# Routing of the last block in fewer stages and ahead of other work, shared weights in ten loads, all layer 2 keys ahead of layer 1's norm

## The chip, the cores and the metric

The kernel runs on one core of a Trainium2 chip. The metric is the device time of one execution in microseconds (us). The core has a matrix engine (TensorE, PE in the profile; PEld is its loading of weights), a vector engine (VectorE, DVE), a scalar engine for activation functions (ScalarE, ACT), GpSimd (POOL) and a sync engine (SP) that here issues most of the DMA transfers. Each engine runs its own instructions in order and waits on semaphores for the others.

## The reference

The input x is f32 of 16 sequences of 128 tokens with 256 features; a context of the same shape feeds the attentions. Four layers follow one another, each a gated cross-attention and a gated feed-forward part:

```
x = x + tanh(g_xattn[i]) * attention_i(layernorm(x), context)
x = x + tanh(g_ffn[i])   * ffn_i(layernorm(x))
```

Three of the feed-forward parts choose 2 of 8 experts for every token (a mixture of experts, MoE). Cut to what matters:

```python
# layer 0: gelu experts, 256 -> 1024 -> 256
gate = softmax(x @ w_gate.T);  scores, idx = top_k(gate, 2)
out  = sum over the two of  scores * (gelu(x @ W1[e] + b1[e]) @ W2[e] + b2[e])
# layer 1: one dense layer with low-rank additions weighted by a softmax
# layer 2: like layer 0 with swiglu experts of 512, chosen by softmax + gate_b, and
#          a shared expert that every token goes through
# layer 3: silu(x @ gate[e]) * (x @ up[e]) @ down[e], weights of the two normalised
```

## The kernel before, in words

**Tiles and blocks.** A sequence (128 tokens) fills the 128 partitions. Four sequences form a block, so there are four blocks, 0 to 3 (`NBLK = 4`, `BPB = 4`, `B = 16`).

**Routing.** `Moe.front` (L436) is the routing of one block: the norm (`ln_block` L316, with `inverse_sd` L221 for 1/sd and `normalized` L299), transposes of the normalised rows (`ps_ln`, L329), the router's product (L413), a softmax, the first choice and the second (`first_max`, each some six DVE operations on 128x32), their sum `both` (L464), two matmuls that rank the tokens of each expert (L469, L470), the weights of the choices (L476 to L502), the row numbers (`off` to `xi`, L505 to L521) and eight scatters by POOL of rows into a table in HBM (`xg`, L524). The running count of tokens per expert, `self.carry`, goes from block to block. `plan` (L592) then works out which expert each slot of 128 rows belongs to; SP reads it into registers (L714).

**Slots.** A slot of an MoE loads 128 rows (`xr`, L753) and, when the expert is a new one, its weights (`fetch`, L1374); without a new expert the load is issued and skipped. PE transposes the rows (L786), does the first products (L1421 in layer 0, L1598 in layer 2, L1646 in layer 3), then the second (L823), and the result is scattered by POOL (L835). Layer 0 does its first slots from a plan of blocks 0 and 1, layer 3 from a plan of blocks 0 to 2, while the attention of later blocks is still going on; the rest come from block 3's plan.

**The order by hand.** `attend` (L1303) emits the work of PE, ACT and DVE in an order written out by hand (`tc.manual_schedule`); the queues of SP and POOL are ordered by a planner. Routing, keys and the like are generators (`jobs`). At each `tick()` every job whose count has run out does its next stage; a stage ends at a `yield n`, and n is the number of ticks until the next one. Once the last scores are out, `late` is true and n is cut to 1, unless it is a `Firm` number, which is kept. At that point the `filler` begins too: early slots in layers 0 and 3, the shared expert of blocks 0 to 2 in layer 2 (`shared2`, L1522; products L1533 and L1555). The filler comes last at every tick. The routing of block 3 is the job that starts last (`jobs.append` after the last `att.output`) and runs beside it.

```python
        def tick():
            for job in list(jobs) + filling:
                job[1] -= 1
                if job[1] <= 0:
                    try:
                        n = next(job[0])
                        job[1] = n if isinstance(n, Firm) else min(n, most[late])
```

**Keys and shared weights.** Layers 1 and 2 run in one `attend`. The keys of both (`keys`, L1144; product L933, eviction by ACT at L1152) need only the context. Ahead of layer 1's first norm stand keys of layer 1's blocks 0 and 1 and of layer 2's blocks 0, 1 and 2; layer 2's block 3 is made with layer 1's next block. The four key tiles of layer 2 and the five tiles of the shared expert's weights use five buffers of one pool (`shared_tile`, L1505), so a weight's load waits until the scores of its buffer's keys are done. `load_shared` starts these five loads of 512 KB in the first step of layer 2's last block.

Of the kernel before, what the change touches and what calls it, by code (L numbers as in the profile page):

```python
# [12 lines left out]
ALU = mybir.AluOpType  # L13
# [6 lines left out]
P = 128  # L20
B = 16
# [69 lines left out]
def kernel(ctx: ExitStack, tc: tile.TileContext, a: dict, out: bass.AP):  # L91
# [112 lines left out]
    class Firm(int):  # L204
        pass

    def quick(job):

        for n in job:
            yield min(n, 3)  # L210
# [105 lines left out]
    def ln_block(blk, see=None, own_set=False):  # L316


        mv, rstd = yield from ln_residual(blk, own_set=own_set)
        if see is not None:  # L320
            see(rstd)
        xns = yield from normalized([xs[b] for b in block(blk)], mv, rstd)
        yield Firm(3) if own_set else 4
        xt = xtpool.tile([P, KC, TB], F32, tag="xnT", name="xnT")
        for pair in range(BPB // 2):
            ps = ps_x.tile([P, KC, 2 * S], F32, tag="x", name="ps_ln")
            for j in range(2):
                for k in range(KC):
                    nc.tensor.transpose(  # L329
                        ps[:, k, j * S:(j + 1) * S],  # L330
                        xns[:, pair * 2 + j, k * P:(k + 1) * P], ident,
                    )
            nc.scalar.copy(xt[:, :, pair * 2 * S:(pair + 1) * 2 * S], ps)
            yield 1 if pair == 0 else 3
        return xns, xt

    def gated_bias(bias_row, gate):
# [34 lines left out]
    def small(tag, w=NE):  # L372
        return rpool.tile([P, BPB, w], F32, tag=tag, name=tag)
# [48 lines left out]
    class Moe:  # L422
# [4 lines left out]
        def __init__(self, layer, wg, turn, see=None):  # L427
            self.layer, self.wg, self.turn, self.see = layer, wg, turn, see
            self.carry = region
            self.done = None  # L430
            self.scatters, self.returns, self.weighted = [], [], []

        def kept(self, shape, tag, dtype=F32):
            return rpool.tile(shape, dtype, tag=tag, name=tag, bufs=NBLK)

        def front(self, blk, plan=None):  # L436
# [25 lines left out]
            first_max(hot[:, 1], key2)  # L462
            both = small("both")
            nc.vector.tensor_tensor(both, hot[:, 0], hot[:, 1], ALU.add)  # L464
            yield Firm(2) if own_set else 6


            ps = ps_x.tile([P, 2, BPB, NE], F32, tag="x", name="ps_rank")
# [31 lines left out]
            )  # L500
            nc.vector.tensor_copy(xns[:, :, D + 1], cg[:, 1])
            nc.vector.tensor_tensor(xns[:, :, D + 2], cg[:, 0], cg[:, 1], ALU.subtract)  # L502
            yield 3
            off = small("off")
            nc.vector.tensor_copy(off[:, 0], self.carry)  # L505
            for i in range(1, BPB):
# [2 lines left out]
            nc.vector.tensor_tensor(  # L509
                self.carry, off[:, BPB - 1], ps[:, 1, BPB - 1], ALU.add  # L510
            )
            at = small("at")
            nc.vector.tensor_tensor(at, off, ps[:, 0], ALU.add)
            where = rpool.tile([P, 2, BPB, NE], F32, tag="where", name="where")
# [11 lines left out]
                        out_offset=bass.IndirectOffsetOnAxis(ap=xi[:, j, i:i + 1], axis=0),  # L526
                    ).ins, self.scatters, "scatter")
            if plan is not None:
                yield 1
                yield from plan()  # L530
            return xnT

        def last(self, pool):
# [55 lines left out]
                )  # L589
            made.append(ins)  # L590

        def plan(self, turns, early=False, kind=""):  # L592

# [2 lines left out]
            def t(shape, tag, dtype=F32):  # L598
# [1 line left out]

            have = t([P, NE], "have")
            nc.vector.scalar_tensor_tensor(
                have, self.carry, float(1 - P if early else 0), region, ALU.add, ALU.subtract
            )
            full = t([P, NE, B], "past")
            nc.vector.tensor_tensor(
# [15 lines left out]
                cnt = left  # L622
            else:
                nc.vector.tensor_scalar(skip, cnt, -1.0, float(B), ALU.mult, ALU.add)
            yield 1
            part = t([P, NE, NE], "part")
            nc.vector.tensor_tensor(
                part, below, cnt[:, None, :].to_broadcast([P, NE, NE]), ALU.mult
# [5 lines left out]
                past, iota[:, :n, None].to_broadcast([P, n, NE]),  # L634
                end[:, None, :].to_broadcast([P, n, NE]), ALU.is_ge,
            )
            yield 1
            eid = t([P, n], "eid")
            nc.vector.tensor_reduce(eid, past, AX.X, ALU.add)
            nc.vector.tensor_tensor(  # L640
# [1 line left out]
            )  # L642
            ahead = t([P, n], "ahead")
            nc.vector.tensor_reduce(ahead, past, AX.X, ALU.add)
            yield 1
            plan = t([P, 4, n], "plan")

            nc.vector.tensor_scalar(plan[:, 0], eid, float(NE - 1), None, ALU.min)
# [5 lines left out]
            else:  # L654
                nc.vector.tensor_tensor(at, ahead, iota[:, :n], ALU.add)
            nc.vector.tensor_scalar(plan[:, 1], at, float(P), None, ALU.mult)
            yield 1

            nc.vector.tensor_tensor(
                plan[:, 2, 1:], plan[:, 0, 1:], plan[:, 0, :n - 1], ALU.not_equal  # L660
# [8 lines left out]
            nc.vector.tensor_copy(plan_i, plan)  # L669
            code = t([P, n], "code" + kind)  # L670
            nc.vector.tensor_scalar(code, plan[:, 0], -1.0, float(NE), ALU.mult, ALU.add)
            yield 1
            if early:

                upto = t([P, NE], "upto")
# [423 lines left out]
    class Fast16:  # L1099
# [30 lines left out]
        def prepare(self, blk, before):  # L1130


            made = [self.queries(blk, before)]
            if blk not in self.kT:
                made.append(self.keys(blk))
            if self.others is not None:

                if blk == 0:
                    made.append(self.keys(1))
                for later in (0, 1, 2) if blk == 0 else (3,) if blk == 1 else ():  # L1140
                    made.append(self.others.keys(later))
            return made

# [156 lines left out]
        mybir.EngineType.PE, mybir.EngineType.Activation, mybir.EngineType.DVE  # L1300
    }

    def attend(parts, most=(99, 1), filler=None, open_end=False):  # L1303

# [27 lines left out]
        with tc.manual_schedule(engines=IN_ORDER):  # L1334
            ln_exp()
            prepared = ahead(*blocks[0][:2], 0)
            for n in range(len(steps) + 2):
                if n == len(steps) - 1 and open_end:
                    next(filler)
                if n == len(steps):  # L1340
                    late = True
                    if filler is not None:
                        filling.append([filler, 0])
                if n < len(steps):
                    if n % BPB == 0:

                        while any(job in jobs for job in prepared):
                            tick()
                        if n // BPB + 1 < len(blocks):
                            att, before, _, blk = blocks[n // BPB + 1]  # L1350
                            prepared = ahead(att, before, blk)
                    att, b = steps[n]
                    att.scores(b, tick)
                if 1 <= n <= len(steps):
                    att, b = steps[n - 1]
                    att.values(b, tick)
                if n >= 2:
                    att, b = steps[n - 2]
                    att.output(b, tick)
                    if b % BPB == BPB - 1:  # L1360
                        _, _, behind, blk = blocks[(n - 2) // BPB]
                        jobs.append([behind(blk), 0])
            while jobs or (filling and not open_end):
                tick()

# [139 lines left out]
    def shared_tile(pool, name):  # L1505
        return pool.tile([P, KC, TB], F32, tag="shared", name=name, bufs=5)

    def shared_weights(pool):

        sw = []  # L1510
        for name in ("l2_w1", "l2_w3"):
            for half in range(2):
                t = shared_tile(pool, "sw")
                nc.sync.dma_start(
                    out=t, in_=a[name][NE, :, half].rearrange("(k p) f -> p k f", p=P)
                )
                sw.append(t)
        w2 = shared_tile(pool, "sw2").rearrange("p k (c d) -> p (k c) d", d=D)
        nc.sync.dma_start(out=w2, in_=a["l2_w2"][NE].rearrange("(c p) d -> p c d", p=P))
        return [*sw, w2]  # L1520

    def shared2(weights, bias, blk, xnT, get):  # L1522

# [563 lines left out]
    def layers(fast):  # L2087
# [11 lines left out]
        def right(stack, name):  # L2099
            return stack.enter_context(tc.tile_pool(name=name, bufs=1, side="right"))  # L2100
# [3 lines left out]
        def routed(moe, turns, begin=None):  # L2104


            plans = []

            def make(blk):
                early = blk < NBLK - 1  # L2110
                kind = str(len(plans)) if early else ""
                plans.append((yield from moe.plan(turns[blk], early, kind)))
                if early and begin is not None:
                    begin(plans[-1])

            def behind(blk):
                if blk in turns:
                    job = moe.front(blk, lambda: make(blk))
                    yield from quick(job) if blk < NBLK - 1 else job
                else:  # L2120
                    yield from moe.front(blk)

            return behind, plans

        def cycle(lanes, n, at=0):
            return [lanes[(at + i) % len(lanes)] for i in range(n)]

        bufs0 = {"xr": 6, "hT": 2, "bias": 2}
        with tc.tile_pool(name="context", bufs=1) as cpool, ExitStack() as for_mid:
# [100 lines left out]

            plans = []

            def load_shared(blk):

                if blk == NBLK - 1:
                    sw.extend(shared_weights(spool))
                yield 1

            def front2(blk):
                def make():  # L2240
                    plans.append((yield from moe2.plan(cycle((2, 1, 0), NSLOT))))

                xnTs.append((yield from moe2.front(blk, make if blk == NBLK - 1 else None)))

            with tc.tile_pool(name="mid", bufs=2) as pool:
                lora = Lora(pool, wpool, biases["base_b"])
# [12 lines left out]
                else:  # L2259
                    parts = [shifted(pool, layer, w, ctxT) for layer, w in zip((1, 2), ws)]  # L2260
                parts = [
                    (parts[0], lambda blk: moe.fetch(pool, blk), lora.run),
                    (parts[1], load_shared, front2),
                ]

                def most_shared():
# [7 lines left out]
                        yield from shared2(sw, biases["sb"], blk, xnTs[blk], get)  # L2274

                if fast:
                    attend(parts, filler=most_shared())
                else:
                    for att, before, behind in parts:
                        general(att, None if att.layer == 2 else before, behind)  # L2280
        with ExitStack() as for_last:
            with tc.tile_pool(name="ffn2", bufs=2) as pool:
                if not fast:
                    sw.extend(shared_weights(right(for_shared, "shared")))
                get = tiles(pool, BUFS2)
                with for_shared, tc.tile_pool(name="hidden", bufs=2) as hpool:
                    def get_shared(tag, shape):
# [150 lines left out]
```

## Time and profile before

| | us |
|---|---|
| median of 11 runs (lowest, highest) | 1657.24 (1654.4, 1660.22) |
| the profiled execution | 1658.69 |
| its span, first to last instruction | 1656.8 |
| mean granted TensorE clock | 0.971 of full speed |

| stretch, us from the start | what runs | PE busy | clock | DMA share |
|---|---|---|---|---|
| 0 to 150 | layer 0 attention | 126.2 of 150 | 0.94 | 0.57 |
| 150 to 235 | block 3's routing, early slots, hand-over | 78.8 of 85 | 0.98 | 0.73 |
| 235 to 415 | layer 0's slots | 180.0 of 180 | 1.00 | 0.42 |
| 415 to 716 | layer 1, layer 2 attention | 281.3 of 301 | 0.96 | 0.14 |
| 716 to 870 | shared expert, block 3's routing, hand-over | 149.6 of 154 | 1.00 | 0.22 |
| 870 to 1480 | layer 2's slots, layer 3 attention | 598.5 of 610 | 0.99 | 0.23 |
| 1480 to 1560 | block 3's routing, early slots, hand-over | 65.1 of 80 | 0.91 | 0.55 |
| 1560 to 1657 | layer 3's slots, end | 60.0 of 97 | 0.83 | 0.61 |

All times are those of one profiled execution. "Busy" is the time in which an engine was at work, the clock is what the throttle granted to TensorE in that stretch, and the DMA share is the mean busy share of the core's 16 DMA engines. In lines of a timeline, the number in brackets is how long the engine had been idle before, and after the arrow stands what ended that wait.

### The profile page before, as it was taken

To read this page: it belongs to the slowest core of one execution; us is meant where nothing else is said; L and a number is where in the kernel's file an instruction comes from. 1 tells how busy PE (TensorE), PEld (TensorE's weight loads), DVE (VectorE), ACT (ScalarE), POOL (GpSimd) and SP (SyncE) were. 2 spreads that over 40 slices of the span, in tenths; PEclk is the share of its full clock that TensorE was granted. 3 is DMA by queue.
4 is the path that set the end of the run, shared out by engine and by line. 5 is a ranking of instruction groups with operands and counts; after the bars stand their busy time and mean duration, and the time that the engine had idled before them with its cause. 6 is when DMAs were issued, how large, how long until landed. Compare 5 with 4: busy or idle time off the path is not lost.

```text
span 1656.8 us, 34913 instructions
## 1 busy us (share of the span) xinstructions
PE 1539.5 (93%) x12803; PEld 1193.2 (72%) x12803; DVE 875.8 (53%) x2850; ACT 637.5 (38%) x1517; POOL 327.8 (20%) x412
## 2 busy tenths in 40 slices
PE   6988999999889999999999999999989999998891
PEld 4677889999455666655559999999846665677791
DVE  3776322422367766764445555556724535557664
ACT  4545423345355555453225333334443323222110
POOL 4133411111600000221100111011150002023433
PEclk9999999999999999999999999999999999999996
DMA  9606575342600000110065413310260000034855
GB/s 340 229 31 221 175 259 177 120 145 89 118 2 1 1 14 15 40 40 26 26 208 161 151 43 135 121 33 28 97 121 1 14 1 27 1 119 135 275 181 174
DMA packets 111272, 169.68 MB, mean 102 GB/s; under 512 B 17129, under 2 KB 84526, under 8 KB 111088
## 3 DMA queue, kind: packets, MB, share of 16 engines
q1 hardware_dynamic: 86224, 112.38, 21.6%
q0 software_dynamic: 20304, 49.66, 9.6%
q10 hardware_dynamic: 4560, 5.25, 1.0%
q8 instruction: 108, 1.77, 0.4%
q14 instruction: 76, 0.62, 0.1%
HBM read 268.81 MB, written 48.18 MB: 191 GB/s over the span
## 4 chain that ended last, share of the span: by engine, by line
PE 76%; DVE 10%; DMA 6%; ACT 4%; issue 1%; POOL 1%; SPq 1%; DVEq 0%; ACTq 0%
PE ps_w L1598 16%; PE ps_e L823 12%; PE ps_h L1421 7%; PE ps_w L1533 6%; PE ps_qk L1855 4%; PE ps_v L1964 3%; PE ps_o L1267 3%; PE ps_s L1212 2%; PE ps_g L1646 2%; PE ps_k L933 2%; DVE rs L1278 2%; PE ps_q L933 2%; PE ps_u L1646 2%; PE ps_s L1985 2%; PE ps_y L2031 2%; PE ps_s L1555 2%
## 5 line engine op out<-in xcount | busy, mean ns | idle before, releaser
L1598 PEld LDWEIGHTS ps_w<-xT,w 128*128 128x128 f32 x2304 | 264.0, 192 | 2.5
L1598 PE MATMUL ps_w<-xT,w 128*128 128x128 f32 x2304 | 264.9, 275 | 0.0
L835 POOL DMA_INDIRECT yd<-y,to x117 | 119.5, 1021 | 561.0 <-DVE c L798 306.6
L823 PE MATMUL ps_e<-w,hT 128*128 128x256 f32 x848 | 197.6, 380 | 2.4 <-DVE hT L1503 1.3
L823 PEld LDWEIGHTS ps_e<-w,hT 128*128 128x128 f32 x848 | 154.5, 190 | 21.6 <-DVE hT L1503 2.3
L1606 ACT ACTIVATE u<-ps_w,b 128x128 f32<-128x128 f32 x312 | 89.4, 368 | 172.3 <-PE ps_w L1598 165.0
L1609 DVE SCALAR_TENSOR_TENSOR m<-ps_w,b,u 128x128 f32<-128x128 f32 x312 | 87.8, 344 | 111.0 <-PE ps_w L1598 94.0
L1421 PE MATMUL ps_h<-xT,w 128*128 128x128 f32 x1120 | 133.5, 278 | 7.1 <-DMA w<-in_l_w_dram 4.3
L1421 PEld LDWEIGHTS ps_h<-xT,w 128*128 128x128 f32 x1120 | 131.4, 194 | 10.5 <-issue 3.7
L1426 ACT ACTIVATE hT<-ps_h,b 128x128 f32<-128x128 f32 x312 | 89.3, 374 | 114.5 <-issue 79.5
L524 POOL DMA_INDIRECT xg<-xn,xi x96 | 94.3, 983 | 153.7 <-ACT u L1539 55.0
L1533 PE MATMUL ps_w<-xnT,sw 128*128 128x512 f32 x256 | 111.9, 593 | 0.0
L831 DVE SCALAR_TENSOR_TENSOR y<-ps_e,c,bias 128x256 f32<-128x256 f32 x78 | 37.6, 482 | 125.7 <-PE ps_e L823 124.5
L1081 POOL TENSOR_TENSOR sum_range<-sum_range,rs 128x256 f32<-128x256 f32 x48 | 35.2, 733 | 342.1 <-DVE rs L1278 156.7
L1533 PEld LDWEIGHTS ps_w<-xnT,sw 128*128 128x128 f32 x256 | 47.9, 190 | 57.3 <-issue 50.9
L1278 DVE RECIPROCAL rs<-ps_o 128x256 f32<-128x256 f32 x32 | 56.2, 1756 | 44.6 <-PE ps_o L1267 43.1
L788 DVE COPY xT<-ps_xr 128x256 f32<-128x256 f32 x117 | 48.5, 417 | 58.3 <-PE ps_xr L786 58.2
L306 ACT ACTIVATE xn<-x,nmr,rstd 128x256 f32<-128x256 f32 x128 | 67.8, 597 | 29.2 <-DVE nmr L302 29.2
L1212 PE MATMUL ps_s<-qM,kT 32*128 32x256 f32 x768 | 71.2, 431 | 5.1 <-ACT e L1227 5.0
L1227 ACT ACTIVATE e<-ps_s 128x512 f32<-128x512 f32 x128 | 65.7, 601 | 12.1 <-PE ps_s L1212 12.0
L815 ACT ACTIVATE bias<-b,c 128x256 f32<-128x256 f32 x78 | 40.4, 518 | 70.5 <-DVE c L801 26.5
L1212 PEld LDWEIGHTS ps_s<-qM,kT 32*128 32x128 f32 x768 | 40.8, 194 | 33.5 <-issue 19.0
(276 smaller groups left out, 2580.2 us busy)
## 6 DMA issues: line engine op xcount, KB each, us to landing
w<-in_l_w_dram SPq DMA_DIRECT2D x156, 1024.0 KB
w<-in_l_w_dram SPq DMA_DIRECT2D x39, 512.0 KB
kT<-in_l_wgu_dram SPq DMA_DIRECT2D x39, 512.0 KB
xg<-zeros POOLq DMA_DIRECT2D x15, 1170.0 KB, 24.8
xr<-xg SPq DMA_DIRECT2D x78, 130.0 KB
b<-in_l_b_dram SPq DMA_DIRECT2D x78, 128.0 KB
kT<-in_l_w_dram SPq DMA_DIRECT2D x39, 256.0 KB
x<-yd POOLq DMA_DIRECT2D x48, 128.0 KB, 4.8
```

The costliest lines, as they stand in the source:

```text
L306: nc.scalar.activation(xns[:, i, 0:D], src, AF.Identity, bias=nmr[:, i:i + 1], scale=rstd[:, i:i + 1])
L524: self.unordered(nc.gpsimd.indirect_dma_start(out=xg[:, :], in_=xns[:, i, :], in_offset=None, out_offset=bass.IndirectOffsetOnAxis(ap=xi[: ...
L823: nc.tensor.matmul(po, lhsT=hT[:, f, :], rhs=lane(s)["w2"][:, f, :], start=(f == 0), stop=(f == nf - 1),)
L835: self.unordered(nc.gpsimd.indirect_dma_start(out=yd[:, :], in_=y, in_offset=None, out_offset=bass.IndirectOffsetOnAxis(ap=to[:, 0:1], axi ...
L1212: nc.tensor.matmul(pss[j][:, 2 * c:2 * c + 2, :], lhsT=self.kT[blk][part, c, tok], rhs=self.qM[blk][part, c, :, tok], start=True, stop=True,)
L1278: nc.vector.reciprocal(rs, po[:, 1])
L1421: nc.tensor.matmul(ps[:, i, :], lhsT=w["w1"][:, k, f * P:(f + 1) * P], rhs=xT[:, k, :], start=(k == 0), stop=(k == KC - 1),)
L1426: nc.scalar.activation(hT[:, f, :], ps[:, i, :], AF.Gelu, bias=w["b1"][:, f:f + 1])
L1533: nc.tensor.matmul(ps, lhsT=wt[:, k, f * P:(f + 1) * P], rhs=xnT[:, k, :], start=(k == 0), stop=(k == KC - 1),)
L1598: nc.tensor.matmul(ps[:, f, :], lhsT=wt[:, k, s, f * P:(f + 1) * P], rhs=xT[:, k, :], start=(k == 0), stop=(k == KC - 1),)
L1606: nc.scalar.activation(u[:, f, :], pair[0][:, f, :], AF.Identity, bias=w["b1"][:, i:i + 1])
L1609: nc.vector.scalar_tensor_tensor(m1[:, f, :], pair[1][:, f, :], w["b3"][:, i:i + 1], u[:, f, :], ALU.add, ALU.mult,)
```

## The change

1. In layers 0, 2 and 3 block 3's routing goes through `rush`: it stops only at `Firm` yields, so the stages between them run in one tick. Which yields are firm, and how long, changes with it. Block 3 may now overtake block 2, so counters (`counted`, `settled`) keep the row counts and the plans in order, and the running count goes to `plan` as an argument.
2. When the routing of the last block of the whole `attend` starts, it is put at the head of the jobs instead of the tail, so that each tick does its stage first.
3. The shared expert's weights are a job of their own that begins at step 24 (the first step of layer 2's last block, as before). It issues ten loads of 256 KB, one per five ticks, instead of five of 512 KB at once.
4. Layer 2's keys of block 3 are put ahead of layer 1's first norm with the others.

```diff
+    def rush(job):
+        while True:
+            try:
+                n = next(job)
+            except StopIteration as end:
+                return end.value
+            if isinstance(n, Firm):
+                yield n
...
@@ ln_block
-        yield Firm(3) if own_set else 4
+        yield Firm(2) if own_set else 4
...
-            yield 1 if pair == 0 else 3
+            yield 1 if pair == 0 else Firm(1) if own_set else 3
@@ Moe.front
-            yield Firm(2) if own_set else 6
+            yield Firm(1) if own_set else 6
...
-            yield 3
+            yield Firm(1) if own_set else 3
+            while self.counted < blk:
+                yield Firm(1)
             off = small("off")
...
+            self.counted += 1
+            carry = self.carry
...
             if plan is not None:
-                yield 1
-                yield from plan()
+                yield Firm(1)
+                while self.settled < blk:
+                    yield Firm(1)
+                yield from plan(carry)
+            self.settled += 1
@@ Moe.plan (the same at each of its yields)
-            yield 1
+            yield Firm(1)
@@ Fast16.prepare
-                for later in (0, 1, 2) if blk == 0 else (3,) if blk == 1 else ():
+                for later in range(NBLK) if blk == 0 else ():
                     made.append(self.others.keys(later))
@@ attend
+                if n in loads:
+                    jobs.append([loads[n], 0])
...
-                        jobs.append([behind(blk), 0])
+                        at = 0 if n == len(steps) + 1 else len(jobs)
+                        jobs.insert(at, [behind(blk), 0])
@@ shared_weights
-                nc.sync.dma_start(
-                    out=t, in_=a[name][NE, :, half].rearrange("(k p) f -> p k f", p=P)
-                )
                 sw.append(t)
+                for k in range(KC):
+                    nc.sync.dma_start(
+                        out=t[:, k, :], in_=a[name][NE, k * P:(k + 1) * P, half]
+                    )
+                    yield 5
...
-        nc.sync.dma_start(out=w2, in_=a["l2_w2"][NE].rearrange("(c p) d -> p c d", p=P))
-        return [*sw, w2]
+        sw.append(w2)
+        for c in range(0, NF2, 2):
+            nc.sync.dma_start(
+                out=w2[:, c:c + 2, :],
+                in_=a["l2_w2"][NE, c * P:(c + 2) * P].rearrange("(c p) d -> p c d", p=P),
+            )
+            yield 5
@@ routed, behind
-                    yield from quick(job) if blk < NBLK - 1 else job
+                    yield from quick(job) if blk < NBLK - 1 else rush(job) if fast else job
@@ layer 2
-                if blk == NBLK - 1:
-                    sw.extend(shared_weights(spool))
...
+                    job = moe2.front(blk, make)
+                    xnTs.append((yield from rush(job) if fast else job))
...
-                    attend(parts, filler=most_shared())
+                    attend(parts, filler=most_shared(), loads={
+                        B + 2 * BPB: shared_weights(spool, sw)
+                    })
```

## Prediction

> **What bounds the kernel now.** I read the busy shares and the chain of waits first, then the timelines of PE, ACT and DVE around each place where the diff changes an order, then SP's waits and the windows with the granted clock.
>
> ```profile
> PE 1539.5 (93%) x12803; PEld 1193.2 (72%) x12803; DVE 875.8 (53%) x2850; ACT 637.5 (38%) x1517; POOL 327.8 (20%) x412
> PE 76%; DVE 10%; DMA 6%; ACT 4%; issue 1%; POOL 1%; SPq 1%; DVEq 0%; ACTq 0%
> ```
>
> TensorE is busy 93% of 1656.8 us, and no matmul is added or removed. So the change can only alter PE's gaps, some 117 us in all, and the granted clock just after them. The routing of a last block, which the change hurries, meets PE here in layer 0:
>
> ```profile
> 150.51 3.81 PE L1421 MATMUL ps_h<-xT,w 128*128 128x128 f32 x32 [1.55 <-DVE x L366]
> 154.15 0.31 PE L469 MATMUL ps_rank<-both,tri 128*128 128x32 f32 x2
> ...
> 192.99 5.47 PE L1421 MATMUL ps_h<-xT,w 128*128 128x128 f32 x32 [2.34 <-DMA w<-in_l_w_dram]
> ```
>
> Columns: start, duration, engine, line, tiles, count, and in brackets the idle time before. The rank matmuls of block 2 followed the filler without a gap. The third line shows the clock: 32 such matmuls take 3.6 to 3.8 us, here 5.47 after a gap of 2.34. The windows say why (time, PE, PEld, DVE, ACT and POOL busy, PEclk, DMA):
>
> ```profile
> 195.00:196.00 1.00, 1.00 (x7) 1.00 (x7) 0.88 (x5) 0.40 (x2) 0.50 (x1) 0.50 0.49 179
> 198.00:199.00 1.00, 1.00 (x10) 0.95 (x9) 0.29 (x1) 0.51 (x2) 0.93 (x1) 1.00 0.37 133
> ```
>
> The granted clock fell to 0.50 for some 3 us. The same followed gaps of 2.53 (432.9: layer 1's first ps_q took 6.32 for 3.44), 3.61 and 4.31 us; none followed gaps of 1.62, 1.77 and 1.98. A gap over some 2.3 us therefore costs itself plus 1.9 to 2.9.
>
> **Layer 0: block 3's normalisation enters ahead of block 2's second choice.** With the instruction lists of both kernels side by side, DVE now does ve, nt, nt, rstd, nmr (L229, 237 to 240, 302) of block 3 between the copy at L458 of block 2 (ends 152.20) and block 2's second first_max, whose eight operations up to both run 152.14 to 153.68, 1.54 us. PE's rank matmuls wait for both. But nt waits for ACT:
>
> ```profile
> 153.49 0.19 DVE L464 TENSOR_TENSOR both<-hot 128x32 f32<-128x32 f32 x1
> 155.58 0.16 DVE L237 SCALAR_TENSOR_TENSOR nt<-r,ve 128x4 f32<-128x4 f32 x1 [0.24 <-ACT r L234]
> ```
>
> The same stretch on ACT:
>
> ```profile
> 152.65 1.14 ACT L1426 ACTIVATE hT<-ps_h,b 128x128 f32<-128x128 f32 x4
> 153.81 1.28 ACT L288 ACT_TABLE_LOAD   x1
> 155.11 0.21 ACT L232 ACTIVATE lv<-ve 128x4 f32<-128x4 f32 x1
> ```
>
> r cannot end before 155.54, because ACT evicts the filler's hT until 153.79 and loads a table for 1.28. nmr ends at 156.33, both at 156.33+1.54 = 157.9, and the rank starts 3.8 us later than 154.15. Behind the waiting rank stand the slot's transposes and ps_e, so PE has nothing else. (+3.8; in addition the clock, 0 to +2.5, taken as the 1.9 of the 5.47 against 3.57.) Next, block 3's own routing runs in one go: from the end of its router, DVE needs 3.45 us to both (0.66 for logits and softmax's start, 2.8 for two first_max and the rest), and the order puts only half an h, 1.79 us, between: +1.7. Moved PE work (transposes, router, rank) cancels.
>
> In return block 3's plan is done at about 180 instead of 210.8. What this is worth at the hand-over is small: SP waited 1.5 us for the plan (below), and all gaps of PE there are 0.56+0.74+1.77 = 3.1. So −1.5 to −3.1, taken as −2.3. The gap at 192.99 stays: its weights, issued at 184.38, took 8.56 us to land. Layer 0: 3.8+1.9+1.7−2.3 = **+5.1** (ends 3.8+0+1.7−3.1 = +2.4 and 3.8+2.5+1.7−1.5 = +6.5).
>
> ```profile
> SPq L1514 <- PE ps_s L1212: 257.5, 3, 190.0
> SPq L714 <- DVE code L671: 88.3, 1, 88.3
> ```
>
> These are SP's waits between 412 and 880 us: for what, total, times, longest. Between 180 and 240 the line for L714 says 1.5.
>
> **Layer 2.** The order on PE becomes: ps_ln of block 3, rank of block 2, one filler product, router, one product, rank of block 3, then the shared expert's second matmul (L1555). Whatever rank waits for, the filler behind it on PE waits too. Before:
>
> ```profile
> 742.16 0.38 PE L469 MATMUL ps_rank<-both,tri 128*128 128x32 f32 x2 [1.62 <-DVE nt L237]
> ...
> 752.36 0.70 PE L1555 MATMUL ps_s<-sw,hTs 128*128 128x256 f32 x2 [1.35 <-DVE hTs L1503]
> ```
>
> ACT can load the table at 736.89, so nmr is done near 739.4, the four xn near 741.55 and, with the filler's m (0.75) and block 2's second choice (1.5) behind it on DVE, both at 744.5: PE idles 2.5 us after the transposes. Block 3's router to both takes 4.3 to 4.7 us with the filler's DVE work, against 3.44 of L1533 in between: 1.0 to 1.4. The last hTs then stands behind off to xi (1.75): PE idles 2.4 to 3.0 instead of 1.35. L1555 resumes near 758.5 rather than 752.36: +6.15, of which 0.88+1.70+0.36 = 2.94 is PE work that only moved: +3.2. Add the clock of one gap (1.9): **+5.1**; ends +3.2 (none) and +6.6 (two gaps). Nothing comes back: after the plan PE is continuous from 792 to 868, SP had the plan at 801 and first waited until 834.87 for buffers (27.5 us on hTs, 6.3 on ps_s), not for the plan.
>
> **Layer 3.** Here the old order has the larger holes:
>
> ```profile
> 1506.87 1.18 PE L329 MATMUL ps_ln<-ident,xn 128*128 128x128 f32 x4 [4.31 <-ACT xn L306]
> 1507.84 1.92 PE L1646 MATMUL ps_g<-xT,kT 128*128 128x128 f32 x8
> ...
> 1525.00 0.38 PE L469 MATMUL ps_rank<-both,tri 128*128 128x32 f32 x2 [1.33 <-DVE both L464]
> ...
> 1557.15 1.13 PE L1646 MATMUL ps_g<-xT,kT 128*128 128x128 f32 x8 [1.98 <-DMA kT<-in_l_wgu_dram]
> ```
>
> Gap 4.31, slow clock behind it 2.5 (1.92 and 1.91 for 1.06 each, and the rest), 1.33 at the rank, and at the hand-over 0.27+1.36+0.96+0.35+1.98 = 4.9 since block 3's scatters end only at 1543.8 (POOL) and xr is issued at 1546.85: 13.0 in all. New: the first ps_g after the normalisation can start at 1505.1, a gap of 2.5; the rank of block 3 waits 2.3 (both at 1511.9); DVE is then full until 1520.4, since the weights, off to xi and block 2's plan (1.26) stand ahead of the filler's hT, so ps_u waits 2.7 to 4.5, say 3.6; scatters end near 1530 and the hand-over is free. 2.5+2.3+3.6 = 8.4, so **−4.6**. Ends: −13 if every hole closes, 0 if SP loses it: block 2's plan comes at 1520 rather than 1511.4, SP issues the tenth xr at 1520.7 for 1514.14, with all later weight loads queued behind it.
>
> **Keys.** Block 3's two ps_k groups (1.88 at 445.29, 1.98 at 447.74) leave layer 1's first scores and join the ten ahead of its norm, at 1.72 each by the rows of L933. ACT's lv stands behind the evictions (0.69 each) and comes 3.44 later, but PE is at work in that time. 3.44−3.86 = **−0.4**; the gap of 2.53 stays. Ends: +3.4 if the first scores were limited elsewhere, −3.9 if the gap shrinks as well.
>
> **Ten pieces.** SP issues in 0.37 us each, five more issues: 1.9 if nothing hid them. But SP waited 257.5 us here for key buffers, stands idle until 834.87, and w2's issue at 709.05 preceded the filler's start at 716.54. Two early w_att loads (layer 1) pass only idle time near 162 us. **0** (−0.5 to +1.9).
>
> **A rule against the trace.** The Trainium skill, "TensorE: Matmul & The Clock Gate", section "What's actually happening", halves the clock only after an idle window of about 3.4 us, which is free-running; here gaps of 2.34 and 2.53 already brought 0.50. By the page alone layer 2's 2.5 us gap would cost no clock (+3.2 instead of +5.1) and the total would be near +3.3. "ScalarE: Activation LUTs", section "What ACT_TABLE_LOAD costs", adds a drain of 1380 ns to a load of 1283; here lv starts 0.02 us after the load's 1.28, so I charge no drain; with it layer 0 would lose 1.4 more.
>
> **Sum.** 5.1+5.1−4.6−0.4+0 = +5.2. On the profiled execution (1656.8 span, 1658.69 with the 1.9 around it) that gives 1663.9; it stood 1.45 above the median of the runs, 1657.24, so the forecast is **1662.4**.
>
> **Rivals.** (1) Faster: layer 3 pays for everything. If its holes nearly all close (−12) and layers 0 and 2 come in at their low ends (+2.4, +3.2), 1657.24−12+5.6−0.4 = 1650.4. It decides once layer 3 returns over 9 us. For it: 4.9 us of hand-over waits there are all late scatters. Against: DVE is full after the routing. (2) It cancels: low ends and my layer 3: 2.4+3.2−4.6−0.4 = +0.6, 1657.8; also what comes if the waits merely change places and the plan lies no nearer to any transfer, that is, the change does not do what its words say. For it: layer 2's hand-over did not wait for the plan at all, and layer 0's by 1.5 us only. (3) Worse: layer 3's gain lost to SP's late tenth xr, clock lost everywhere: 6.5+6.6+0−0.4 = +12.7, 1669.9.
>
> **How the numbers follow.** 0.2% of 1657 is 3.3 us, about what a measurement of this kernel can tell from no change. Forecast 0.45 (its own range 1659 to 1668), rival 1 0.25, rival 2 0.20, rival 3 0.10. Slower 0.45+0.10 = 0.55, same 0.20, faster 0.25. The range leaves out half of rival 3 and the faster part of rival 1: 1652.5 to 1669.5.
>
> **What would show it.** Right: a gap of 3 to 4 us before the rank of block 2 near 154 with 0.50 clock after; a new gap of about 2.5 before the rank near 744; the 4.31 gap near 1502 halved, scatters of layer 3 ending before 1532, no waits on xg after it; L933's ps_k with 48 matmuls in a row near 416. Wrong: DVE taking block 2's choice before nt; PE filling these gaps with other filler; or SP late near 1520 and new weight waits behind it.

## The result, and the profile after

The changed kernel takes 1682.08 us (median of 8 runs, 1674.96 to 1685.58) against 1656.16 of the kernel before (30 runs, 1654.37 to 1660.91). The ratio is 1.0146, with a 95% interval of 1.0133 to 1.0160: some 24 us slower. The forecast was 1662.4, range 1652.5 to 1669.5: the right sign, and less than a quarter of the size. The profiled execution has a span of 1681.0 us, 24.2 more than before.

The page's busy line and its chain of waits:

```profile
PE 1549.1 (92%) x12803; PEld 1204.4 (72%) x12803; DVE 876.9 (52%) x2850; ACT 636.8 (38%) x1517; POOL 327.5 (19%) x412
DVE 1%; DMA 1%; SPq 0%; issue 0%
```

The same 12,803 matmuls cost 9.6 us more PE time, and PE stood idle 131.9 us instead of 117.3. The chain, traced back from the end, covers only the last 2% here and tells nothing. So I cut both traces at the same instructions. "Idle" is the length of a stretch less PE's busy time in it; "busy" counts the same matmuls in both, so its difference is mostly the clock:

| stretch (first and last instruction) | before, us | after, us | idle | busy |
|---|---|---|---|---|
| layer 0: last filler product before block 2's rank, to the last ps_e | 265.2 | 277.3 | +6.2 | +5.9 |
| layer 1, and layer 2's attention | 300.8 | 299.8 | +2.6 | −3.6 |
| layer 2: first shared product to first slot product | 152.6 | 159.2 | +2.9 | +3.8 |
| layer 3: first ps_g to last ps_e | 138.0 | 143.4 | +2.8 | +2.7 |

The three routing stretches hold 24.1 of the 24.2 us; in layer 1's stretch more idle time and less time at a lowered clock nearly cancel. In layer 0 both forecast waits are there, on PE (start, duration, line, tiles, count, idle before):

```profile
159.87 0.63 PE L480 MATMUL ps_rank<-both,tri 128*128 128x32 f32 x2 [3.93 <-DVE both L475]
...
161.20 5.94 PE L841 MATMUL ps_e<-w,hT 128*128 128x256 f32 x16
...
175.14 0.38 PE L480 MATMUL ps_rank<-both,tri 128*128 128x32 f32 x2 [1.76 <-DVE sm_s L398]
...
175.83 5.30 PE L841 MATMUL ps_e<-w,hT 128*128 128x256 f32 x16
...
206.33 5.44 PE L1443 MATMUL ps_h<-xT,w 128*128 128x128 f32 x32 [3.46 <-DMA w<-in_l_w_dram]
```

A ps_e of this count takes 3.62 us at full clock; here they took 5.94 and 5.30. The windows (columns: stretch, length, busy time and count of PE, PEld, DVE, ACT and POOL, then PEclk, DMA share, GB/s) show the clock at 0.50 for some 6 us behind the first wait:

```profile
160.00:162.00 2.00, 2.00 (x8) 1.88 (x9) 1.68 (x9) 1.97 (x3) 0.00 (x0) 0.50 0.00 0
166.00:168.00 2.00, 2.00 (x16) 1.82 (x15) 0.78 (x4) 0.00 (x0) 0.06 (x1) 1.00 0.00 0
```

The cause on DVE is the one foretold, block 3's nt ahead of block 2's second choice:

```profile
157.61 0.16 DVE L247 SCALAR_TENSOR_TENSOR nt<-r,ve 128x4 f32<-128x4 f32 x1 [3.61 <-ACT r L244]
...
159.62 0.19 DVE L475 TENSOR_TENSOR both<-hot 128x32 f32<-128x32 f32 x1
```

In layer 2, PE shows the three waits and the slow clock behind the first (eight filler products 6.31 us, later 3.68):

```profile
757.05 0.64 PE L480 MATMUL ps_rank<-both,tri 128*128 128x32 f32 x2 [2.37 <-DVE both L475]
...
757.92 6.31 PE L1562 MATMUL ps_w<-xnT,sw 128*128 128x512 f32 x8
...
770.80 0.38 PE L480 MATMUL ps_rank<-both,tri 128*128 128x32 f32 x2 [1.34 <-DVE off L518]
...
774.78 0.70 PE L1584 MATMUL ps_s<-sw,hTs 128*128 128x256 f32 x2 [2.01 <-DVE hTs L1525]
```

In layer 3 the hole before the norm's transposes shrank from 4.31 to 3.06 us and no hole over 0.5 us is left at the hand-over, but there is a hole that was in no sum:

```profile
1520.76 2.16 PE L339 MATMUL ps_ln<-ident,xn 128*128 128x128 f32 x8 [3.06 <-ACT xn L316]
...
1531.05 0.50 PE L480 MATMUL ps_rank<-both,tri 128*128 128x32 f32 x2 [2.75 <-DVE both L475]
...
1541.39 1.98 PE L1675 MATMUL ps_g<-xT,kT 128*128 128x128 f32 x8 [2.27 <-issue]
...
1552.80 0.66 PE L804 MATMUL ps_xr<-ident,qT 128*128 128x128 f32 x2 [6.67 <-DMA qT<-xg]
```

PE waits 6.67 us for rows of the tenth slot. SP knew that slot's place at 1539, yet issued its load at 1550.54, behind the last of block 3's eight scatters (1547.97 on POOL). The next three fences are SP's timeline, POOL's timeline, and SP's waits from 1510 to 1580:

```profile
1550.54 0.35 SPq L771 DMA_DIRECT2D qT<-xg  x1
```

```profile
1539.12 0.96 POOL L539 DMA_INDIRECT xg<-xn,xi  x1 [0.78 <-issue]
...
1547.97 0.96 POOL L539 DMA_INDIRECT xg<-xn,xi  x1 [0.30 <-issue]
```

```profile
SPq L771 <- DMA xg<-xn,xi: 11.0, 1, 11.0
...
SPq L732 <- DVE done L697: 9.2, 1, 9.2
```

The code says why. An early plan ends with `return plan_i, code, order, list(self.scatters), early`, and the loads of its slots wait for every scatter in that list. Hurried, block 3 has put its own scatters into the list before block 2's plan ends. The slots of blocks 0 to 2 then wait for rows that they don't need.

### The profile page after: what moved, and what is told of

The parts are those of the page before. It is cut to its first block, busy times and chain, and to the rows that moved or that the text cites. A ratio compares the mean times of both kernels' runs of the same rounds, so it can differ in the third digit from the quotient of the medians.

```text
span 1681.0 us, 34933 instructions
## 1 busy us (share of the span) xinstructions
PE 1549.1 (92%) x12803; PEld 1204.4 (72%) x12803; DVE 876.9 (52%) x2850; ACT 636.8 (38%) x1517; POOL 327.5 (19%) x412
## 5 line engine op out<-in xcount | busy, mean ns | idle before, releaser
L1627 PE MATMUL ps_w<-xT,w 128*128 128x128 f32 x2304 | 265.0, 275 | 0.0
L841 PE MATMUL ps_e<-w,hT 128*128 128x256 f32 x848 | 202.0, 385 | 2.5 <-DVE hT L1525 1.9
L1448 ACT ACTIVATE hT<-ps_h,b 128x128 f32<-128x128 f32 x312 | 89.2, 372 | 117.3 <-issue 83.5
L1884 PE MATMUL ps_qk<-kvx,w_att 128*128 128x512 f32 x128 | 62.7, 623 | 0.6 <-DVE kvx L1871 0.6
```

Source lines behind the costliest of these rows:

```text
L841: nc.tensor.matmul(po, lhsT=hT[:, f, :], rhs=lane(s)["w2"][:, f, :], start=(f == 0), stop=(f == nf - 1),)
L1448: nc.scalar.activation(hT[:, f, :], ps[:, i, :], AF.Gelu, bias=w["b1"][:, f:f + 1])
L1627: nc.tensor.matmul(ps[:, f, :], lhsT=wt[:, k, s, f * P:(f + 1) * P], rhs=xT[:, k, :], start=(k == 0), stop=(k == KC - 1),)
```

## The experiments

Unless said otherwise, each is the changed kernel with the edits shown. `RUSH` and `FIRST` name the layers in which block 3's routing has fewer stages, and those in which it stands at the head of the jobs:

```diff
-                    yield from quick(job) if blk < NBLK - 1 else rush(job) if fast else job
+                    yield from quick(job) if blk < NBLK - 1 else rush(job) if fast and moe.layer in RUSH else job
...
-                        at = 0 if n == len(steps) + 1 else len(jobs)
+                        at = 0 if first and n == len(steps) + 1 else len(jobs)
```

Outside `RUSH` the `Firm` numbers are those of the kernel before as well. Lengths of the three stretches of the table above, in us, from one profiled execution each (two kernels with the same order in a stretch differ by up to 1.8 in layer 2 and 4 in layer 3, in part because the clock behind the remaining waits falls or does not):

| kernel | layer 0 | layer 2 | layer 3 | ratio to before, 95% interval |
|---|---|---|---|---|
| before | 265.2 | 152.6 | 138.0 | |
| changed | 277.3 | 159.2 | 143.4 | 1.0146 [1.0133, 1.0160] |
| keys and ten loads alone | 265.0 | 154.3 | 137.2 | 1.0007 [0.9993, 1.0022] |
| and hurried in layer 0 | 277.3 | 152.6 | 134.0 | 1.0069 [1.0043, 1.0095] |
| and hurried in layer 2 | 264.3 | 159.6 | 137.4 | 1.0037 [1.0022, 1.0051] |
| and hurried in layer 3 | 265.2 | 152.6 | 143.9 | 1.0051 [1.0029, 1.0073] |
| fewer stages, at the tail | 271.9 | 161.2 | 147.8 | 1.0142 [1.0117, 1.0167] |
| all stages, at the head | 263.6 | 152.7 | 133.3 | 0.9970 [0.9954, 0.9986] |
| the same, timed again | 263.5 | 154.4 | 133.9 | 0.9988 [0.9972, 1.0004] |
| layer 3, scatters held back | 265.0 | 154.3 | 145.0 | 1.0029 [1.0012, 1.0045] |
| layer 0, 30 and 15 idle matmuls | 274.1 | 152.6 | 137.3 | 1.0044 [1.0029, 1.0059] |
| layer 0, 16 and 7 idle matmuls | 272.5 | 152.6 | 137.2 | 1.0028 [1.0016, 1.0041] |
| before, place at the head | 263.8 | 154.4 | 134.2 | 0.9985 [0.9974, 0.9996] |
| place at the head in layer 3 alone | 266.1 | 152.6 | 133.5 | 0.9988 [0.9973, 1.0002] |

**Part by part.** `RUSH = FIRST = ()`, then `(0,)`, `(2,)`, `(3,)`:

> Only the keys and the ten loads are changed; the last block's routing runs as in the kernel before. Theory (the loss sits wholly in the routing): within 0.2% of before, 1653 to 1658 us; lined up by matmul number the two traces showed 1 to 3 us won between layer 1's first keys and the shared expert. Rival (the two key groups ahead of layer 1's norm delay the first scores by the whole 3.4 us, and ten issues cost SP): 1659 to 1662.

> Keys and ten loads, and the hurried routing in layer 0 alone. Theory (two waits of DVE, 3.9 and 1.8 us, and the lowered clock after both, 3.1 and 1.7, none of it given back at the hand-over): 11 to 13 us above the run with keys and loads alone, about 1667. Rival (the clock after a wait is chance, and much of the 12 us came from the weights' DMA at the hand-over): 4 to 7 above, about 1661.

> Keys and ten loads, and the hurried routing in layer 2 alone. Theory (the three waits at the ranks and at hTs and one lowered clock): 4 to 6 us above the run with keys and loads alone, about 1660. Rival (part of layer 2's 5 us is the shift that layer 0 hands on): 0 to 2 above.

> Keys and ten loads, and the hurried routing in layer 3 alone. Theory (the tenth slot's rows now wait for block 3's eight scatters, 6.7 us of idle PE with the clock lowered behind it): 5 to 8 us above the run with keys and loads alone, about 1662. Rival (layer 3 wins 4 to 5 us as forecast, and only the shift from layers 0 and 2 spoils it): 1650 to 1652.

Measured medians: 1658.51, 1667.43, 1663.14 and 1664.16 us against 1657.34. Keys and loads alone can't be told from nothing. Above them, by the ratios, layer 0 costs 0.62%, layer 2 0.30%, layer 3 0.44%. With 0.07% for keys and loads that adds up to 1.43%, and the whole change measured 1.46%. So the parts add up within their intervals (layer 0's, from four runs, is the widest), and there is no sign that one borrows from another. Layer 0 came out at 9 to 10 us rather than 11 to 13, nearer to the theory than to its rival; the other two as expected. The rival that layer 3 wins and is only spoilt from outside falls: alone it still loses, with the same waits of 3.07, 2.75, 2.28 and 6.77 us.

The moved keys in the kernel with keys and loads alone, on PE:

```profile
416.15 20.76 PE L954 MATMUL ps_k<-ctxT,w_att 128*128 128x512 f32 x48
439.45 2.16 PE L341 MATMUL ps_ln<-ident,xn 128*128 128x128 f32 x8 [2.53 <-ACT xn L318]
...
451.50 0.86 PE L1233 MATMUL ps_s<-qM,kT 32*128 32x256 f32 x4
```

From the first key product to the third group of scores it is 35.35 us, before it was 35.79 (415.57 to 451.36). That is the −0.4 of the forecast, with the gap of 2.53 unchanged, but the match is luck: behind that gap layer 1's first ps_q took 5.79 us here and 6.32 before. Without these 0.5 us of clock the moved keys gain nothing.

**Stages or place.** `FIRST = ()` with `RUSH = (0, 2, 3)`, and the reverse:

> The changed kernel, but block 3's routing starts at the tail of the jobs as before; the fewer stages stay in all three layers. PE's order is that of the changed kernel; on DVE block 2's second choice is ahead of block 3's norm again. Theory (the place at the head costs layer 0's first wait and its clock, 3.9 and 3.1 us; everything else comes from the fewer stages): about 7 below the changed kernel, 1674 to 1676, layer 0's second wait of 1.8 and layer 3's of 6.7 still there. Rival (the place does most of the harm): under 1664.

> Block 3's routing at the head of the jobs, but with all its stages as before. PE's order is that of the kernel before. Theory (the fewer stages set the order of PE's waits; the place alone only swaps a few DVE instructions): 1657 to 1660, level with keys and loads alone. Rival (the place does most of the harm): over 1665.

Both missed in an instructive way. Fewer stages at the tail took 1681.89 us, as slow as the changed kernel. Layer 0's first wait is gone, as the theory said, and with it the slow clock there. The second shrank to 0.59 us, yet the clock fell all the same, from 164.6 to 171.5, behind a gap of 0.81 us; the 16 matmuls of the last line take 1.95 us at full clock:

```profile
154.39 0.31 PE L483 MATMUL ps_rank<-both,tri 128*128 128x32 f32 x2
...
155.01 3.62 PE L844 MATMUL ps_e<-w,hT 128*128 128x256 f32 x16
...
162.09 1.95 PE L425 MATMUL ps_router<-wgl,xnT 128*128 128x8 f32 x16 [0.81 <-ACT xnT L345]
163.90 3.10 PE L1446 MATMUL ps_h<-xT,w 128*128 128x128 f32 x16
```

In all that gave 5.4 us in layer 0. But layers 2 and 3 gave it back: there the wait before block 2's rank grew from 2.37 to 4.51 us and the one before block 3's transposes (layer 3) from 3.06 to 4.76, with block 3's routing behind the other jobs. The 6.67 us wait for rows stays (6.29). So the fewer stages cost about as much with either place.

All stages at the head of the jobs took 1651.25 us against 1656.99, faster than before, and timed again 1654.62 against 1655.9. Neither the theory (level) nor the rival (slower) had this.

**The rows of the tenth slot.** Hurried in layer 3 alone, with row numbers and scatters held back:

```diff
                 xrs[s] = xr
+                self.loaded = s + 1
...
+            while rushed and self.layer == 3 and self.loaded < full_slots(NBLK - 1):
+                yield Firm(1)
             off = small("off")
```

> Hurried routing in layer 3 alone, but its row numbers and scatters are held back until the loads of all 17 early slots are issued. Theory (the tenth slot's rows waited for block 3's scatters, which the list handed over with block 2's plan now holds): the 6.7 us gap and its clock go, the waits at the hand-over come back (about 5 us); 1657 to 1660, so 4 to 6 below the hurried layer 3. Rival (SP is late because block 2's plan itself is late): a gap of over 4 us before the tenth slot stays, 1662 to 1665.

SP issued the tenth slot's load 25 us ahead of the first of block 3's scatters (1548.64), and PE has no gap over 1 us there:

```profile
1523.46 0.34 SPq L777 DMA_DIRECT2D qT<-xg  x1
```

SP still waited 7.8 us for block 2's plan there (8.9 in the hurried layer 3), but no longer 11 us for scatters. So the hole came from the scatters in the list, and not from the late plan. But the time hardly fell: 1662.38 us, 1.8 below the hurried layer 3 and not the 4 to 6 expected (the profiled execution, 1668.89, is the slowest of its ten, so the table's 145.0 is high). The scatters now end so late that the hand-over waits 2.33, 4.88 and 1.06 us, with the clock lowered behind it:

```profile
1562.27 0.69 PE L811 MATMUL ps_xr<-ident,qT 128*128 128x128 f32 x2 [4.88 <-DMA qT<-xg]
```

Letting the tenth load pass block 3's scatters wasn't tried: a read and writes of the same table would then have no order between them.

**Idle time and the clock.** The hurried layer 0 with matmuls that do nothing in front of the two ranks:

```diff
+            if run["fast"] and self.layer == 0 and blk >= 2:
+                for _ in range(30 if blk == 2 else 15):
+                    nc.tensor.matmul(
+                        ps.rearrange("p j b e -> p (j b e)"), lhsT=ident,
+                        rhs=ident[:, 0:2 * BPB * NE], start=True, stop=True,
+                    )
```

> Hurried routing in layer 0 alone, with 30 and 15 idle matmuls (identity on identity, into the ranks' own PSUM tile, overwritten by the ranks) just ahead of the two ranks that wait. Theory (the throttle answers to PE's idleness): PE's waits shrink to under 1 us each, the clock stays at 1.00 behind them, the ranks start no later, and 3 to 5 us come back: 1662 to 1664. Rival (the slow ps_e behind the waits has another cause, such as the weights' DMA or DVE): clock and time as in the hurried layer 0, 1667.

> The hurried layer 0 with about half as many idle matmuls, 16 and 7, so that they fill the two waits without outlasting them (the 30 and 15 took 6.7 and 3.3 us for waits of 3.5 and 1.8). Theory (idle time sets the clock): clock 1.00 behind both waits, ranks no later than without them, 1 to 4 us below the first filled run, 1661 to 1663. Rival (shorter filling leaves gaps enough for the clock to fall): 1665 to 1668.

The first took 1664.64 us, just above its expectation: the filling lasted 6.7 us for a wait of 3.5, so part of the gain was spent. The second took 1661.63, 5.8 below the hurried layer 0 (1667.43), at the low end of its expectation. On PE, first the hurried layer 0 without filling, then the second of these kernels, and the clock behind:

```profile
159.36 5.95 PE L844 MATMUL ps_e<-w,hT 128*128 128x256 f32 x16
```

```profile
155.77 3.68 PE L485 MATMUL ps_rank<-ident 128*128 128x64 f32 x32
159.50 0.41 PE L489 MATMUL ps_rank<-both,tri 128*128 128x32 f32 x2
...
160.22 3.62 PE L850 MATMUL ps_e<-w,hT 128*128 128x256 f32 x16
```

```profile
160.00:162.00 2.00, 2.00 (x13) 1.79 (x13) 1.28 (x7) 1.97 (x5) 0.00 (x0) 1.00 0.00 0
```

The rank starts 7.4 us after the filler product, as without the idle matmuls (7.3), and ps_e is back at 3.62 instead of 5.95 us. In the traces layer 0's stretch is 4.8 us shorter (277.3 to 272.5), about what the two ranks and ps_e behind the waits gained. So a large part of what layer 0 lost is clock, 5.8 of 9 to 10 us by the medians and 4.8 of 12.3 by the traces, and at these two waits it is PE's idleness that lowers it.

**The place alone.** The kernel before with the one edit of `jobs.insert` (the other parts of the change switched off), the place in layer 3 alone, and the earlier kernel again:

> The same kernel as the one with the place at the head and all stages kept, timed again. Theory (block 3's normalisation no longer waits behind block 2's stages in layer 3, so PE's 4.3 us gap there halves): 0.2 to 0.4% faster than before, 1650 to 1654. Rival (the first measurement of seven runs was chance): within 0.1%.

> The kernel before with one edit: block 3's routing at the head of the jobs. No keys moved, no loads split, no stages fewer. Theory (the gain is the place alone, in layer 3): as the run with keys and loads, within 2 us of it, 1650 to 1654. Rival (the gain needs the moved keys or the split loads): 1655 to 1658.

> Keys and ten loads, all stages kept, the place at the head in layer 3 alone. Theory (the gain is layer 3's): within 1 us of the run with the place in all layers. Rival (layer 0 gives 1 to 2 us of it): 1 to 2 us slower than that.

The medians are 1654.62, 1654.61 and 1653.11 us against 1655.9 of 35 runs. The second timing of the first kernel did not reach the expected 0.2 to 0.4%, and its interval takes in no change; the place alone gives 0.15% with an interval just clear of nothing (0.04 to 0.26%), between its theory and its rival. The three can't be told apart by their times. The trace of the place alone shows the gap that shrank, in layer 3, before block 3's transposes (4.31 us before):

```profile
1506.66 0.99 PE L341 MATMUL ps_ln<-ident,xn 128*128 128x128 f32 x4 [2.42 <-DVE xT L809]
```

The wait at block 3's rank falls from 1.33 to 0.53. The length of the stretch alone would prove nothing, since 134.0 us came without the new place too. But PE's idle time in it is 8.5 to 9.6 us in the four kernels with this place and all stages, and 10.8 to 13.0 in the six with layer 3's old order. The place alone is the version that beats both kernels, by some 2 us (0.7 to 4.3 by the interval) over the kernel before.

## Why the prediction was wrong

The sum was +5.2 and the profiled execution shows +24.2. Step by step:

- **Layer 0's two waits** were right: 3.8 forecast, 3.93 measured; 1.7 forecast, 1.76 measured.
- **Layer 0's clock** was mis-sized: taken once, as 1.9, it measured +5.9. I charged it to the first wait alone and took the bound of 2.3 us from three gaps of 1.6 to 2.0 that had gone unpunished. The trace of the kernel before already spoke against it, further from the routings: its clock fell to 0.50 behind gaps of 1.87 (before 491.13), 1.66 (521.74) and 1.84 (682.24). Here the clock fell to 0.50 behind a gap of 1.76 too, and behind the waits for weights at 206.33 (3.46) and 240.11 (1.95). Filling the two routing waits gave back 4.8 us of the stretch.
- **Layer 0's hand-over** failed as a step: −2.3 was forecast for the earlier plan. SP's wait for the plan did go, but SP then waited for buffers (on ps_e, 47.9 us in all against 34.3 between 150 and 235), and the gap before the weights grew from 2.34 to 3.46 us. "Moved PE work cancels" was part of that: before, block 3's rank ran directly ahead of this gap. That this work had filled the wait for weights is argued from the trace; no run isolates it.
- **Layer 2** had its mechanism right, and its clock at half: +3.2 of waits against +2.9 measured, 1.9 of clock against +3.8. Nothing came back at its hand-over, as forecast.
- **Layer 3** is the step that failed most: −4.6 forecast, +5.4 measured. Its three named waits were sound (2.5, 2.3 and 3.6 forecast; 3.06, 2.75 and 2.27 measured), the free hand-over too. What I left out was the list of scatters that block 2's plan hands to its loads. I followed SP's tenth load only to the plan that it reads (forecast some 9 us late, and about so it was), and not to the writes that it waits for: 6.67 us. The lowered clock behind the old hole was to vanish, 2.5; instead 2.7 more came, for four waits over 2 us stand where one stood.
- **Keys and ten loads**, −0.4 and 0, together can't be told from nothing; the −0.4 itself was met by luck of the clock.

Of the 19 us between forecast and result 11 are clock (4.0 in layer 0, 1.9 in layer 2, 5.2 in layer 3), 6.7 the wait for scatters and 3 the hand-over of layer 0; some 2 us of small gaps that went from layer 3 stand against them. The rival that came closest was the third ("clock lost everywhere and layer 3's gain lost"), at 1669.9, given one chance in ten. It named the late tenth load and the clock, but put the load down to the late plan, and had the size of neither. Given these steps, the right sign is no success: layer 3 alone was forecast to win 4.6 us and lost 5.4.

## What to carry to other kernels

Putting a stage earlier in an order written by hand moves everything that its dependencies are built from: before costing it, follow each load that comes after it to all the writes that it will wait for, not only to the values that it reads. On an engine that is busy 93% of the time, price a new wait as itself plus a chance of half speed for the next 3.4 or 6.8 us, and don't count on a length below which it is free. Fewer and larger stages, as these traces read, take away the places where other work could slip in; giving the late job precedence with its stages kept was the only part of this change that gained, and not much.

## What the runs showed of the hardware

I had not expected the clock to be this sensitive. It fell to 0.50 behind a gap of 1.76 us, and in one kernel behind 0.81 with 16 narrow router products (8 columns each) just after it; whether the throttle takes those for idleness too was not tested. The same gap decides differently from kernel to kernel: 32 matmuls took 5.46 us behind a gap of 1.96 in the one with keys and loads alone, 3.84 behind 1.99 in the one with all stages at the head, and 3.81 behind 2.48 with the place alone.

The slow stretches whose length I took come in steps. From the clock in half microseconds of the changed kernel, the one behind the gap of 1.76 lasted 3.4 us, beginning at 176.1, a microsecond after the gap had ended; the one behind 3.93 lasted 6.8 (159.1 to 165.9), and the one of the 6.67 us hole 10.3 (from 1548.2). By estimate from the first two, half speed costs 1.7 or 3.4 us on top of the gap.

The Trainium skill, "TensorE: Matmul & The Clock Gate", section "What's actually happening", names an idle window of about 3.4 us that is free-running. The free-running part agrees with this spread, and the slow stretches are one, two or three such lengths; a whole idle window does not fit gaps of 1.8 to 2.5 us, and the measurement decides. Idle matmuls, whose result is overwritten, kept the clock at 1.00 behind two waits and were worth 5.8 us by the medians.
